# Masked self-attention over 16 batches on one core: the first batch's work placed by a plan written for it, and a new order at the end of the last batch

## The chip, the cores and the metric
The kernel runs on one core of a Trainium2 chip. The metric is the device time of one execution in microseconds (us), as a median of several runs. TensorE is called PE below, its weight loads PEld, VectorE DVE, ScalarE ACT, GpSimd POOL, and SyncE, which issues most of the transfers, SP.

## The reference
```python
xt = transpose(x, (0, 2, 1))              # x: 16 batches x 512 x 1024 tokens
qh = heads(xt @ Wq.T)                     # 8 heads of 64; queries, keys and values are all qh
scores = 0.125 * einsum('bhqd,bhkd->bhqk', qh, qh)
logits = (scores * cmask + (1 - cmask) * -1e30) * rmask      # one 0/1 mask, by column and by row
ctx = einsum('bhqk,bhkd->bhqd', softmax(logits), qh)
return x + transpose(ctx @ Wo.T, (0, 2, 1))
```
A token whose mask is 0 is no key for anybody. As a query its logits are all 0, so its context is the plain mean of all 1024 values, one row for the whole batch. The masks are drawn with about half the tokens active.

## The kernel before
**What is tiled.** The host hands in x also by token. On the core, the batches are ranked by their number of active tokens, and of each only the active tokens (up to 512, 528 or 544, padded) are gathered, 128 rows at a time, by an indirect transfer on POOL's queue (`rows`, L419). Batch 0 uses 512 columns, batches 1 to 4 use 544, later ones 528, the last two 512. The passive tokens need only the mean of x over all tokens. For it x is loaded once more by channel (`load_half`, `load_all`, L446 and L461) and summed along the tokens, for batches 0 and 1 in eight halves of 128 x 512, by ACT with an accumulator (`sum_half`, L456).

**Precision.** Matrices stand as a high and a low half-precision part, so that a product is three matmuls (high x high, low x high, high x low).

**The steps of a batch.** `xt` (L507) transposes gathered rows on PE; ACT writes the high part xh, DVE the low part xl. `query` (L536) makes a quarter e of q for half g of the tokens, 12 matmuls. ACT copies it out; DVE zeroes padding in place (L554), and `qsplit` (L562) makes the parts hl on DVE, from which four SP transfers build the operand xx (`spread`, L579). `value` (L600) transposes q to v; for batch 0 by PE transposes of q, later by matmuls on xx. The sums of squares of v give a bound on each head's scores: `peaks`, `top`, `bottom` (L656 to L697), with two small PE steps; the exponentials take the negative bound nm as their bias. `scores` (L741) does one pair of heads p for half the rows u, 8 matmuls (16 for a wider batch) into four PSUM banks, then four ACT exponentials that free these banks (L788). `attend` (L795) multiplies by v, 32 recorded matmuls; `recip_sums` and `recip_rows` (L839, L857) make reciprocals of the sums: a PE transpose, a DVE copy to rr (L867), a transfer to DRAM and two broadcasting transfers back into rb. `norm` (L890) multiplies by rb and splits into high and low on DVE. `product`, `project` (L923, L939) multiply by Wo, in units of three matmuls for each pair p, DVE adds x, and POOL scatters the rows to the output (`scatter_now`, L998).

**The order.** One stage of `run` (L1041) holds the scores of one batch, and between them the rest of the batch before and the preparation of the next. Its 18 steps S are the (p, i) of the batch with two empty ones; scores are issued for even i. Work is put between them by `fill` (L1270): from batch 1 on, by a table `plan` of steps; for batch 0, from a list m with costs, dealt out by shares (L1266 to L1281). From batch 1 on PE's order is exactly that of the code (`manual_schedule`, L1181); in batch 0 a scheduler orders PE. ACT and DVE are ordered by the scheduler throughout, and each engine does its instructions strictly in that order. `free` holds further calls by step: loads, sums, reciprocals, normalisations. Before batch 0's scores stands a setup (L1081 to L1153): masks are ranked, Wq and Wo are split (`split`, L183; the low part of Wo in `wide_rest`, L1131), the first rows are gathered, and the first quarters of q and v of batch 0 are made. PE runs dummy matmuls there (`warm`). `permute` (L215) orders the mask of batches 2 to 15 in one go, in batch 0.

**The end.** `last` (L1010) does what is left of the last batch: reciprocals and attention of its last pair 3, `norm_part` for that pair in two halves, and the projection of four chunks of 128 rows. The products of the pairs 0 to 2 are put ahead, as they do not need the last normalisation: 1 + 3 + 3 + 1 units for chunks 0 to 3 before it, then pair 3 of chunks 0 and 1, two units of chunk 3, and pair 3 of chunks 2 and 3. The normalisation of pair 2 is issued by `free` at the last step (L1309).

Of the kernel before, what the change touches and what calls it, by code (L numbers as in the profile page):

```python
# [47 lines left out]
class Fast:  # L48
# [166 lines left out]
    def permute(self, b0, b1):  # L215
# [3 lines left out]
        each = self.sb([P, n, TB, B], F16, "ch", 2)  # L219
# [226 lines left out]
    def load_half(self, b, k, after=None):  # L446

        c, h = k // 2, k % 2
        if k == 0:
            self.source(b)  # L450
        t = self.sb([P, T // 2], F32, *((("xm", 2), ("ub", 3), ("xi", 8), ("xi", 8))[k // 2 if b < 2 else 0]))
        src = self.x_nat[bass.ds(self.st[b]["row"], 1), c * P:(c + 1) * P, h * T // 2:(h + 1) * T // 2].rearrange("o p t -> (o p) t")
        self.once(self.nc.sync.dma_start(out=t, in_=src), after)
        self.st[b]["xm"].append(t)

    def sum_half(self, b, k):  # L456
        s = self.st[b]
        with self.behind(*self.exp):
            self.nc.scalar.activation(s["xm"][k], s["xm"][k], AF.Copy, accum_out=s["ms2"][:, k:k + 1])  # L459
# [397 lines left out]
    def recip_rows(self, b, p):  # L857
# [8 lines left out]
        with self.tc.high_priority(offset=HPO):  # L866
            self.spot_reads += [nc.vector.tensor_copy(rr, pt[:10]).ins] * spot  # L867
# [142 lines left out]
    def last(self, b):  # L1010
# [13 lines left out]
        self.recip_rows(b, 3)  # L1024
        self.attend(b, 3)
        self.attend_tail()
        self.product(s["ch"], s["cl"], chunk(0), pos[0], range(2, 3))
        for i in (1, 2):
            self.product(s["ch"], s["cl"], chunk(i), pos[i], range(3))
        self.product(s["ch"], s["cl"], chunk(3), pos[3], range(1))  # L1030
# [6 lines left out]
        self.product(s["ch"], s["cl"], chunk(3), pos[3], range(1, 3))  # L1037
        for i in (2, 3):
            self.project(b, i, pos[i], range(3, DC))

    def run(self, flag):  # L1041
# [71 lines left out]
        self.warm(13)  # L1113
        for k in range(3):
# [3 lines left out]
        for k in range(2 * DC):  # L1118
            self.load_half(0, k, self.pe)
# [7 lines left out]
        def half1(k):  # L1127
            with self.behind(*[self.last_xx] * (k > 2)):
                self.load_half(1, k, self.beat)

        def wide_rest():  # L1131
            with self.behind(self.last_hl):
                for f in wide:
                    f()
# [10 lines left out]
        first += [(0, index1)] + value(0, 0) + g1[:1] + query(0, 1, 1)[:1] + g1[1:2]  # L1145
        first += [(0, L(self.sum_half, 0, k)) for k in range(2 * DC)]
        first += value(0, 1) + query(0, 2, 0) + g1[2:3] + query(0, 2, 1)[:1] + g1[3:4]
        first += [(0, shift0), (0, wide_rest)]
        for _, f in first:
            f()  # L1150
        with self.behind(self.st[0]["top"]):
            for _, f in query(0, 1, 1)[1:] + query(0, 2, 1)[1:]:
                f()  # L1153
# [11 lines left out]
        def permute():  # L1165
            with self.behind(self.last_hl):
                self.permute(2, B)

        self.paced = True
        begin = g1[4:] + [(1.5, lambda: None)] + query(0, 3, 0) + value(0, 2) + query(0, 3, 1)  # L1170
        begin += xt(1)[:2] + value(0, 3)
        begin += [(0, apart(self.range_x, 0, c)) for c in range(DC)]
        groups = [(2, 4), (4, 8), (8, 11), (11, B - 2), (B - 2, B)]
        todo, carry = [], []
        if True:
            stack = ExitStack()
            for b in range(B + 1):
                o, n = b - 1, b + 1
                if b == 1:
# [21 lines left out]
                if n < B:  # L1201
                    q, x, v = (lambda e, g: query(n, e, g)), xt(n)[2 if b == 0 else 0:], (lambda e: [(0.25, L(self.value, n, e))])
# [7 lines left out]
                    if b:  # L1210
                        pre = [(0, L(self.active, *g)) for g in new[0]]
# [11 lines left out]
                    else:  # L1223
                        m = sums + x + pk(b, 1)
                        for g in new[0]:
                            m += [(0, permute), (0, L(self.active, *g))]
                        m += q(0, 0) + tp(b, 1) + bt(b, 1) + q(0, 1)
                        for g in new[0]:
                            m += [(0.3, L(self.slots, *g))]
                        m += hot + q(1, 0) + q(1, 1) + tc(0) + v(0) + index + take  # L1230
                        m += rng[:2] + tv(0) + rng[2:] + q(2, 0) + v(1)
                        m += q(2, 1) + pk(n, 0) + tp(n, 0) + q(3, 0) + bt(n, 0)
                        m += q(3, 1) + v(2) + tc(1) + [(0, L(self.means, n))]
# [13 lines left out]
                if b == 0:  # L1247
                    m = begin + m
# [12 lines left out]
                if b == 0:  # L1261
                    for k in range(2 * DC):
                        free.setdefault(k // 2, []).append(lambda k=k: half1(k))
                        free.setdefault(3 + k // 2, []).append(L(self.sum_half, 1, k))

                share = [(0, 0) if i is None else ((0, 0.3), (0.4, 0.4), (1.3, 1.3), (1.2, 1.2))[i] for _, i in S]  # L1266
                unit = sum(c for c, _ in m) / sum(map(sum, share)) if b == 0 else 0
                done, goal, pos = 0.0, 0.0, 0

                def fill(st, half):  # L1270
                    nonlocal done, goal, pos
                    if b:
                        for _, f in plan.get((st, half), []):
                            f()
                        return
                    part, end = share[st][half], st == N - 1 and half == 0
                    goal += part * unit
                    while pos < len(m) and (end or (part and done + m[pos][0] / 2 <= goal)):
                        m[pos][1]()
                        done += m[pos][0]  # L1280
                        pos += 1  # L1281

                for st, (p, i) in enumerate(S):
# [14 lines left out]
                    if b == 0 and p == 0 and i == 2 and self.wide[b] > 512:  # L1298
                        self.tail_scores(b, 0)

# [159 lines left out]
```

## Time and profile before
| | us |
|---|---|
| median of 3 runs (979.9, 980.95, 984.29) | 980.95 |
| the profiled execution | 984.38 |
| its span, first to last instruction | 982.7 |
| PE busy | 939.4 |
| DVE busy | 715.4 |
| ACT busy | 650.3 |
| POOL busy | 310.3 |

The busy times are those of the profiled execution. In a row of the timeline stand the start, the time of one or of several merged instructions, engine, line, operation and tiles, and in brackets how long the engine had been idle and what ended that. In a row of windows stand the stretch, its length, an engine's busy time with its number of instructions, the granted clock of PE (1.00 is full), the share of the transfer engines and the rate in GB/s.

### The profile page before, as it was taken

How to read it: one execution, taken by the hardware profiler on the slowest of the kernel's cores; microseconds unless marked ns; L12 is line 12 of the kernel's file. 1: busy time of each engine (PE TensorE's matmuls, PEld its weight loads, DVE VectorE, ACT ScalarE, POOL GpSimd, SP SyncE). 2: the span in 40 equal slices, each digit the busy share in tenths (PEclk: the TensorE clock that was granted, in tenths of full speed). 3: DMA queues.
4: the chain of work that ended last, by engine and by line, in shares of the span. 5: the costliest groups of instructions: out<-in, count | busy, mean ns of one | idle time of the engine just before them, and what ended most of it. 6: DMA issues, size and time to landing. Idle time of an engine off the chain costs nothing. (4 is left out here: it accounts for less than half of the span.)

```text
span 982.7 us, 22820 instructions
## 1 busy us (share of the span) xinstructions
PE 939.4 (96%) x8124; PEld 583.5 (59%) x8124; DVE 715.4 (73%) x2425; ACT 650.3 (66%) x1685; POOL 310.3 (32%) x309
## 2 busy tenths in 40 slices
PE   6787999999999999999999999999999999999997
PEld 4444656656666665666666666666666656565543
DVE  7687676777776786877688777777877678785663
ACT  4777666657766676776767678665767667565651
POOL 2201013124151342505234241432515135243452
PEclk9999999999999999999999999999999999999999
DMA  5747455567566577656657777654757747555552
GB/s 165 226 134 200 111 136 174 163 190 218 129 200 187 180 203 201 208 150 197 185 175 222 198 228 222 179 169 136 205 177 237 221 134 210 136 164 171 162 174 99
DMA packets 79145, 176.30 MB, mean 179 GB/s; under 512 B 14545, under 2 KB 22481, under 8 KB 79025
## 3 DMA queue, kind: packets, MB, share of 16 engines
q1 hardware_dynamic: 57968, 107.09, 38.9%
q0 software_dynamic: 21056, 67.68, 21.9%
q8 instruction: 66, 1.08, 0.5%
q14 instruction: 55, 0.44, 0.1%
HBM read 91.36 MB, written 33.91 MB: 127 GB/s over the span
## 5 line engine op out<-in xcount | busy, mean ns | idle before, releaser
L788 ACT ACTIVATE p<-pss,nm 128x528 f32<-128x528 f32 (+2 forms) x512 | 354.4, 703 | 101.1 <-PE pss L773 92.6
L808 PE MATMUL pss<-p,v 128*64 128x264 f32 (+2 forms) x2048 | 244.9, 392 | 0.0
L773 PE MATMUL pss<-xx 128*128 128x118 f16 (+17 forms) x1856 | 215.9, 290 | 7.8 <-ACT p L788 5.2
L1000 POOL DMA_INDIRECT y_out<-xa,idx x68 | 84.4, 1242 | 413.3 <-DVE nq L685 97.5
L808 PEld LDWEIGHTS pss<-p,v 128*64 128x64 f32 x2048 | 142.3, 138 | 88.6 <-issue 8.4
L773 PEld LDWEIGHTS <-xx 128*128 128x128 f16 (+1 forms) x1856 | 103.0, 97 | 91.3 <-issue 36.4
L547 PE MATMUL pm<-xh,wqh 128*128 128x264 f16 (+5 forms) x512 | 142.3, 278 | 2.7 <-DVE rr L867 0.8
L547 PE MATMUL pm<-xh,wql 128*128 128x264 f16 (+5 forms) x512 | 141.5, 276 | 0.0
L547 PE MATMUL pm<-xl,wqh 128*128 128x264 f16 (+5 forms) x512 | 141.5, 276 | 0.0
L422 POOL DMA_INDIRECT xa<-x_in,idx x68 | 75.7, 1113 | 125.9 <-DMA xx<-hl 47.0
L547 PEld LDWEIGHTS <-wqh 128*128 128x128 f16 x1024 | 97.1, 98 | 30.4 <-issue 11.4
L788 ACT ACTIVATION_READ_ACCUMULATOR p<-pss,nm 128x1 f32 x512 | 105.3, 206 | 0.0
L931 PE MATMUL pm<-woh,ch 128*128 128x512 f16 x240 | 91.1, 380 | 0.0
L931 PE MATMUL pm<-woh,cl 128*128 128x512 f16 x240 | 90.9, 379 | 0.0
L931 PE MATMUL pm<-wol,ch 128*128 128x512 f16 x240 | 90.9, 379 | 0.0
L551 ACT ACTIVATE q<-pm 128x264 f32<-128x264 f32 (+5 forms) x128 | 50.9, 398 | 46.9 <-PE pm L547 46.7
L937 DVE SCALAR_TENSOR_TENSOR xa<-pm,xa 128x512 f32<-128x512 f32 x61 | 41.6, 682 | 48.7 <-PE pm L931 48.1
L1000 POOL DMA_INDIRECT y_out<-xi,idx x60 | 64.6, 1077 | 35.7 <-PE pss L719 14.4
L614 ACT COPY v<-pm 128x512 f32<-128x512 f32 x64 | 37.5, 586 | 55.1 <-PE pm L610 54.3
L931 PEld LDWEIGHTS <-ch 128*128 128x128 f16 x480 | 44.9, 98 | 47.5 <-issue 4.1
L422 POOL DMA_INDIRECT xi<-x_in,idx x60 | 59.2, 986 | 22.5 <-issue 15.2
L459 ACT ACTIVATE xm<-xm 128x1024 f32<-128x1024 f32 (+1 forms) x60 | 62.3, 1041 | 3.6 <-DMA xm<-x_nat_in 3.6
(230 smaller groups left out, 1461.8 us busy)
## 6 DMA issues: line engine op xcount, KB each, us to landing
xm<-x_nat_in SPq DMA_DIRECT2D x56, 512.0 KB
xx<-hl SPq DMA_DIRECT2D x208, 136.0 KB
rb<-rd SPq DMA_DIRECT2D x72, 132.0 KB
xx<-hl SPq DMA_DIRECT2D x48, 128.0 KB
pt<-c SPq DMA_DIRECT2D x36, 132.0 KB
pt<-p SPq DMA_DIRECT2D x36, 132.0 KB
rb<-rd SPq DMA_DIRECT2D x32, 136.0 KB
ub<-ud SPq DMA_DIRECT2D x16, 256.0 KB
```

Of the source, the lines that this page charges most:

```text
L422: dma = self.nc.gpsimd.indirect_dma_start(out=tile[:n], out_offset=None, in_=self.x, in_offset=bass.IndirectOffsetOnAxis(ap=idx, axis=0))
L459: self.nc.scalar.activation(s["xm"][k], s["xm"][k], AF.Copy, accum_out=s["ms2"][:, k:k + 1])
L547: self.beat = nc.tensor.matmul(pq, lhsT=w[:, c, e * P:(e + 1) * P], rhs=xx[:, c, cols], start=(k == 0), stop=(k == 3 * DC - 1)).ins
L551: nc.scalar.activation(s["q"][:, e, cols], pq, AF.Copy, scale=1.0 / (SX * SW))
L614: nc.scalar.copy(v, pv)
L773: m = nc.tensor.matmul(flat[:, c0:c1], lhsT=w, rhs=x, start=banks[n] not in banks[:n], stop=banks[n] not in banks[n + 1:])
L788: e = nc.scalar.activation(t, flat[:, at:at + A], AF.Exp, bias=s["nm"][p // 2][:, p % 2 * 2 + k:p % 2 * 2 + k + 1], scale=SCALE, accum_out ...
L808: mm = nc.tensor.matmul(pav[k * DK:(k + 1) * DK, g], lhsT=s["v"][p][:, i, k * DK:(k + 1) * DK], rhs=ps[k, i][:, cols], start=(i == 3), sto ...
L931: mm = nc.tensor.matmul(po[:cols.stop - cols.start], lhsT=a[:, e, cols], rhs=w[:, e, :], start=(e == 0 and k == 0), stop=(e == DC - 1 and ...
L937: return self.nc.vector.scalar_tensor_tensor(x, po, 1.0 / (SX * SW), x, ALU.mult, ALU.add).ins
L1000: dma = self.nc.gpsimd.indirect_dma_start(out=self.out, out_offset=bass.IndirectOffsetOnAxis(ap=idx, axis=0), in_=x, in_offset=None)
```

## The change
- **Loads and sums of the first two batches.** The halves of x of batch 0 go to buffers of the tag `p` (exponentials). The first four loads of batch 0 wait for nothing on PE. The other four, and the first four of batch 1, are issued after the first transposes of batch 0 instead of after the third; the last four of batch 1 after the spread of batch 0's third quarter. Four of batch 0's sums are called ahead of its values, four after value 1. For batch 1 the sums of halves 4 to 7 are made by DVE (`tensor_reduce`) and not by ACT.
- **Batch 0's order.** It gets a table `plan` like the other batches, PE's order there is that of the code, and its small PE steps use the spare PSUM bank. Quarter 1 of q is split right after value 1.
- **Moved out of batch 0.** `wide_rest` goes to the first four steps of batch 1. `permute` runs for each group of batches at the place where their masks are needed (batches 0, 2, 6, 9 and 12), with its buffer under the tag `hl`.
- **The end.** The normalisation of pair 2 comes after the copy to rr of pair 3 (`self.recip`). Ahead of the last normalisation stand 1 + 3 + 1 units of chunks 0 to 2; after it chunk 2 and then chunk 3 are finished one by one.

```diff
-        each = self.sb([P, n, TB, B], F16, "ch", 2)
+        each = self.sb([P, n, TB, B], F16, "hl", 2)
...
+        t = self.sb([P, C], F32, "p", 12)[:, :T // 2] if b == 0 else \
+            self.sb([P, T // 2], F32, *((("xm", 2), ("ub", 3), ("xi", 8), ("xi", 8))[k // 2]))
...
+            if b == 1 and k > 3:
+                    self.nc.vector.tensor_reduce(s["ms2"][:, k:k + 1], s["xm"][k], AX.X, ALU.add)
+                return
...
+            self.recip = nc.vector.tensor_copy(rr, pt[:10]).ins
...
         self.recip_rows(b, 3)
+        with self.behind(self.recip):
+            self.norm(b, 2)
...
-        for i in (1, 2):
-            self.product(s["ch"], s["cl"], chunk(i), pos[i], range(3))
-        self.product(s["ch"], s["cl"], chunk(3), pos[3], range(1))
+        self.product(s["ch"], s["cl"], chunk(1), pos[1], range(3))
+        self.product(s["ch"], s["cl"], chunk(2), pos[2], range(1))
...
-        self.product(s["ch"], s["cl"], chunk(3), pos[3], range(1, 3))
-        for i in (2, 3):
-            self.project(b, i, pos[i], range(3, DC))
+        self.product(s["ch"], s["cl"], chunk(2), pos[2], range(1, 3))
+        self.project(b, 2, pos[2], range(3, DC))
+        self.product(s["ch"], s["cl"], chunk(3), pos[3], range(3))
+        self.project(b, 3, pos[3], range(3, DC))
...
+        for i in range(DC):
+            self.load_half(0, i)
         for k in range(3):
...
-        for k in range(2 * DC):
-            self.load_half(0, k, self.pe)
+            if k == 0:
+                for i in range(DC, 2 * DC):
+                    self.load_half(0, i, self.pe)
+                for i in range(DC):
+                    self.load_half(1, i, self.pe)
...
-        first += [(0, index1)] + value(0, 0) + g1[:1] + query(0, 1, 1)[:1] + g1[1:2]
-        first += [(0, L(self.sum_half, 0, k)) for k in range(2 * DC)]
-        first += value(0, 1) + query(0, 2, 0) + g1[2:3] + query(0, 2, 1)[:1] + g1[3:4]
-        first += [(0, shift0), (0, wide_rest)]
+        first += [(0, index1)] + sums0[:4] + value(0, 0) + g1[:1] + query(0, 1, 1)[:1] + g1[1:2]
+        first += value(0, 1) + split1 + sums0[4:] + query(0, 2, 0) + g1[2:3] + query(0, 2, 1)[:1] + g1[3:4]
+        first += [(0, shift0)]
...
-                if b == 1:
+                if b == 0:
                     self.spots = True
                     stack.enter_context(self.tc.manual_schedule(engines={mybir.EngineType.PE}))
...
-                        pre = [(0, L(self.active, *g)) for g in new[0]]
+                        pre = [(0, L(f, *g)) for g in new[0] for f in (self.permute, self.active)]
...
+                        plan = {(0, 0): g1[4:] + query(0, 3, 0) + value(0, 2) + rng0,
+                                (3, 0): query(0, 3, 1) + value(0, 3) + pk(b, 1) + x[:1],
+                                (5, 0): x[1:2], (5, 1): x[2:3],
+                                (7, 0): x[3:] + tp(b, 1) + q(0, 0) + bt(b, 1), (8, 1): pre,
+                                (9, 0): q(0, 1), (9, 1): q(1, 0) + post, (11, 0): hot,
+                                (12, 0): q(1, 1) + tc(0) + v(0) + rng[:2], (12, 1): index, (13, 0): take[:3],
+                                (14, 0): tv(0) + q(2, 0) + rng[2:], (14, 1): v(1) + q(2, 1) + pk(n, 0),
+                                (16, 0): q(3, 0) + tp(n, 0) + take[3:], (16, 1): q(3, 1),
+                                (17, 0): bt(n, 0) + v(2) + tc(1) + [(0, L(self.means, n))]}
...
-                            if p < 2 or b == B - 1:
+                            if p < 2:
```
In `plan`, q, x and v are the queries, transposes and values of batch 1, and the others those of batch 0.

62 lines of the change are left out of this document (19 added, 43 removed).

## The prediction
> **What bounds the kernel now.** I read the page first, then PE by stages, then the stage that stands out, then the waits and the timeline in it.
>
> ```profile
> span 982.7 us, 22820 instructions
> ```
> ```profile
> 31.60:105.00 73.40, 57.82 (x435) 0.91 0.60 163
> 105.00:930.00 825.00, 813.75 (x7238) 1.00 0.63 183
> ```
> From 105 to 930 us PE is idle for 11.3 of 825 us: there PE is the bound, and what PE gets done earlier by 105 should stay a gain to the end. From 31.6 (first scores of batch 0) to 105 (end of batch 0's last attention) 73.4 - 57.8 = 15.6 us are idle, and the clock is low. The same stretch by pieces:
>
> ```profile
> 45.40:48.40 3.00, 2.97 (x10) 0.50 0.75 226
> 58.80:62.10 3.30, 3.12 (x10) 0.50 0.57 149
> ...
> 92.90:95.80 2.90, 0.00 (x0) 1.00 0.72 182
> 95.80:102.90 7.10, 6.14 (x34) 0.54 0.36 83
> ```
> Three times PE ran at about half clock. That cost 2.97 x 0.5 + 3.12 x 0.5 + 6.14 x 0.46 = 5.9 us. With 15.6 idle, **21.5 us** is all that can be won there. Who caused the idle time:
>
> ```profile
> PE pss L773 <- ACT p L788: 5.0, 4, 3.1
> ...
> PE pm L670 <- DVE smcol L661: 2.2, 1, 2.2
> ```
> PE waits for exponentials to leave PSUM, for one spread, and for the bound before the first exponential. The chain of waits at the end holds only the last scatter, so the tail is taken from the timeline.
>
> **Part 1, the loads.** Before, SP held the first load until 20.36, behind PE's third transposes.
>
> ```profile
> 20.36 1.21 SPq L453 DMA_DIRECT2D xm<-x_nat_in  x2
> ```
> ```profile
> 16.14 0.60 ACT L477 ACTIVATE xh<-pss 128x512 f16<-128x512 f32 x1 [4.57 <-PE pss L519]
> ```
> In the changed build four loads wait only for their batch's number (about 7.5 us, an estimate), and ACT has four half sums in front of its first xh copy, which began at 16.14. Four loads issued by about 9.7 have 6.4 us to land and be summed. If they are late, all shifts 1:1; early they gain nothing by themselves, as PE's transposes wait for gathered rows. I take 0 (up to 5 lost, by the slowest load of the rows below).
>
> **Part 2, the bound.** The chain to the first exponential:
>
> ```profile
> 29.60 0.57 ACT L614 COPY v<-pm 128x512 f32<-128x512 f32 x1
> ...
> 33.67 0.62 ACT L593 ACTIVATE tmp<-v 128x512 f32<-128x512 f32 x1
> ...
> 37.07 0.69 ACT L788 ACTIVATE p<-pss,nm 128x512 f32<-128x512 f32 x1 [2.78 <-DVE nm L683]
> ```
> Value 1 was out of PSUM at 30.2, but ACT squared it only at 33.67, behind five half sums and two q copies; DVE's reduction, smcol and two PE steps follow. In the changed order the square stands right behind the copy. The copy itself comes 0.5 us earlier (no half sum ahead of q), so the square ends about 30.2, 4.1 us earlier. Then ACT still owes four sums (some 0.63 each, row 51.51 below) and two q copies, until 33.4. First exponential: 33.7, **3.3 us** earlier.
>
> **Part 3, batch 0's plan.** I walk PE through the eight score groups in the changed order, with these durations:
>
> ```profile
> 38.51 0.38 ACT L551 ACTIVATE q<-pm 128x256 f32<-128x256 f32 x1
> 38.77 0.59 ACT L614 COPY v<-pm 128x512 f32<-128x512 f32 x1
> 39.24 0.71 ACT L788 ACTIVATE p<-pss,nm 128x512 f32<-128x512 f32 x1
> ...
> 39.91 0.71 ACT L788 ACTIVATE p<-pss,nm 128x512 f32<-128x512 f32 x1
> ```
> ```profile
> 77.33 3.67 PE L808 MATMUL pss<-p,v 128*64 128x256 f32 x32
> ...
> 83.12 0.28 PE L547 MATMUL pm<-xh,wqh 128*128 128x272 f16 x1
> ...
> 84.40 0.28 PE L547 MATMUL pm<-xh,wql 128*128 128x272 f16 x1
> ```
> So, start to start on ACT, an exponential costs 0.67, a q copy 0.26, a v copy 0.47; on PE an attention 3.67, a query 84.40 - 83.12 + 0.11 = 1.4, and a score group some 1.6. A group may start only when the four exponentials of the one before are out. Idle PE that I find left:
> - Group 1 to 2: ACT needs 1.6 + 4 x 0.67 + 0.26 + 0.47 = 5.0 after the group's start and begins late (33.7); PE has 1.6 + 1.4 + 0.6 to do. Idle 1.5.
> - Group 2 to 3 has a **new wait**: DVE now does batch 1's half sums 4 to 7, and two of them stand ahead of the zeroing of q's last quarter, which value 3 needs; value 3 stands ahead of group 3 on PE. DVE is there at 39.5. Their loads go out behind the third spread, about 38.8 to 40.9. Rows for such a landing:
>
> ```profile
> 45.63 1.91 SPq L453 DMA_DIRECT2D xi<-x_nat_in  x4
> ```
> ```profile
> 51.51 0.63 ACT L459 ACTIVATE xi<-xi 128x512 f32<-128x512 f32 x1 [0.52 <-DMA xi<-x_nat_in]
> ```
> The second of these loads, issued about 46.4, had landed at 51.5: 5.1 us on busy queues. At 2.5 us the second lands at 42, at 5.1 at 44.5. Queued behind on DVE: this zeroing, the split of quarter 3, xl of batch 1. I take 42.4, DVE goes on at 43.0, idle 2.7 (bounds 0.3 and 5).
> - Group 4 to 5: `bottom` on PE now needs a maximum that stands behind two range reductions on DVE. Idle 1.2.
> - Group 6 to 7: fill of only 2.0 (a query, a value, the index) beside 3.5 us of ACT. Idle 1.5.
> - Before value 2 of batch 1, the spread:
>
> ```profile
> 87.12 1.71 PE L773 MATMUL pss<-xx 128*128 128x472 f16 x16
> ...
> 95.87 0.19 PE L610 MATMUL pm<-two,xx 128*128 128x64 f16 x1 [2.98 <-DMA xx<-hl]
> ```
> Before, its query ended where the row 87.12 begins, and the value came 8.8 us later. In the new order PE has 5.1 us of work there (a group, two queries, small steps), since batch 1's first scores moved behind it. At 8.2 us, idle 3.1.
> - Small ones: 0.5.
>
> Sum 10.5. The groups then start at about 31.9, 37.2, 44.2, 50.8, 56.8, 65.4, 70.5 and 79.5, value 2 at 87.4. The clock:
>
> ```profile
> 57.02 0.66 PE L519 MATMUL pm<-ident,xa 128*128 128x128 f32 x4 [1.23 <-DVE xl L478]
> 58.98 2.86 PE L773 MATMUL pss<-xx 128*128 128x512 f16 x8 [1.31 <-ACT p L788]
> ```
> The gaps of 3.1 (longest wait for L788) and 3.0 us (before 95.87), and these two of 1.2 and 1.3 with 0.7 of work between, were followed by half clock; the 2.2 for smcol was not. I count one half-clock spell, after the last gap, as costly as the one there before (2.8). So 13.3 of loss stays of 21.5: **8.2 us won** by 105, the 3.3 of part 2 within it. No row shows this order, so bounds: no spell and half of the gaps, 16; a spell of 2.8 after each of the five, 3 lost.
>
> The Trainium skill, page "TensorE: Matmul & The Clock Gate", section "What's actually happening", has the clock fall to half after one idle window of about 3.4 us. Here gaps of 2.98 and 3.08 us did it, so the trace is harsher. By the page none of the gaps left would do it; that is the first rival.
>
> **Part 4, what left batch 0.** The wide split (4 x 0.6 on DVE) comes back while DVE waits for value 2: 0. `permute`:
>
> ```profile
> 52.94 3.42 DVE L220 TENSOR_TENSOR ch<-c,given 128x1792 f16<-128x1792 f16 x1
> ...
> 60.74 2.00 DVE L223 TENSOR_REDUCE act<-ch 128x112 f16<-128x1792 f16 x1
> ```
> ```profile
> 167.14 0.29 DVE L478 SCALAR_TENSOR_TENSOR xl<-pm,xh 128x128 f16<-128x128 f32 x1 [0.16 <-ACT xh L477]
> ```
> ```profile
> 168.08 0.28 PE L547 MATMUL pm<-xh,wqh 128*128 128x274 f16 x1
> ```
> 3.42 + 2.00 for 1792 columns give 1.55 for 512 in batch 2, with the comparison 1.75; 1.3, 1.3 and 0.9 for the groups of batches 6, 9 and 12. In the build they stand ahead of the last xl (167.14, free at 167.4), which PE wants for the query from 168.2. 1.75 later is a wait of 0.95; with the same slack 0.5, 0.5 and 0.1 follow. DVE has idle time to catch up: I take **1.5 us lost** (0 to 5.2).
>
> **Part 5, the tail.**
>
> ```profile
> 962.73 0.33 PE L862 MATMUL pm<-ident,rcol 128*128 128x128 f32 x1 [0.23 <-DVE rcol L855]
> ```
> ```profile
> 963.05 0.69 DVE L913 TENSOR_TENSOR c<-c,rb 128x512 f32<-128x512 f32 x1 [0.38 <-DMA rb<-rd]
> 963.66 0.27 DVE L867 COPY rr<-pm 10x128 f32<-10x128 f32 x1
> ...
> 968.92 0.76 DVE L881 TENSOR_TENSOR c<-c,rb 128x256 f32<-128x256 f32 x2 [3.54 <-SPq L1430]
> ...
> 970.07 0.41 DVE L888 TENSOR_TENSOR xl<-c,xh 128x256 f16<-128x256 f32 x1
> ...
> 975.32 1.34 DVE L937 SCALAR_TENSOR_TENSOR xa<-pss,xa 128x512 f32<-128x512 f32 x2 [1.25 <-PE pss L931]
> ```
> ```profile
> 966.60 0.39 PE L931 MATMUL pm<-woh,xh 128*128 128x512 f16 x1
> ...
> 971.88 0.38 PE L931 MATMUL pm<-woh,xh 128*128 128x512 f16 x1
> ```
> ```profile
> 977.54 0.96 POOL L1000 DMA_INDIRECT y_out<-xa,idx  x1 [0.30 <-POOLq L1430]
> ```
> The copy to rr could start at 963.1, when the transpose ends, but stood behind the product L913: 0.55 earlier, and so are rb and 968.92. PE is full from 966.6 on, so this moves no end; it pays for the 3 units moved behind. Eight units took 971.88 - 966.60, 0.66 each; five last until 969.9, the third matmul wants the low half at 970.3, and that comes at 970.48 - 0.55. At the end chunks 2 and 3 were added one after the other (975.32, two in 1.34), and the last scatter began only when POOL was through with the one before (0.30 idle on its own queue). Now chunk 2 is added about 974 and its scatter gone; chunk 3's add still ends at 976.66, and its scatter begins 0.3 later, 976.96: 0.6 earlier, perhaps more as it has the transfers alone. **0.8 won** (0.3 to 1.1).
>
> **Sum.** -8.2 + 1.5 - 0.8 = -7.5 us. The profiled execution took 984.38 and would take 976.9; it lies 3.4 above the median of the runs, 980.95. I put the gain on the median: **973.5 us**.
>
> **Rivals.**
> - *The clock stays up* (chance 0.12). No spell of half clock: 2.8 more, 970.7; if the half sums also land before DVE asks, 2.4 more, 968.3. For it: the gaps are shorter than before. Against: three spells in this trace.
> - *New waits take the place* (0.18). The half sums land at 5 us (2.1 more), the following gap gets a half-clock spell (1.5), permute costs all of 5.2: 980.8. For it: the landing of 5.1 us. Against: twelve loads have gone by then, so the queues should hold less.
> - *Slower: PE's clock through batch 0* (0.14). Five gaps are left, and each may start a spell that costs 1.5 to 2.8. The sum is even when the spells cost 10.3, 20 us at half clock; all five at 2.8 give 984.7. For it: a pair of gaps of 1.2 and 1.3 sufficed before. Against: a gap of 2.2 did not.
> - *The change doesn't do what it says* (0.02): loads 0 to 3 land after 16 us and the sums in front of xh stop ACT; at 5 us late, 978.5.
>
> **How the numbers follow.** The forecast has 0.54, its own range 970.5 to 976.5. 966 to 982 takes in the rivals down to part of the third and leaves out some 0.1. A measurement of this kernel tells 0.5%, 4.9 us, from no change: below 976.05 lie most of the forecast and the first rival, 0.62; above 985.9 the worst of the third and what I have not thought of, 0.10; between, 0.28.
>
> **What would show it.** First exponential near 33.7 (part 2). A DVE wait for the loads L462 about 40 (new wait), a PE wait before group 3 released by DVE. Batch 0's last attention ending at about 96 to 97 instead of 104.8. A clock row of half rate only about 87 to 95. Waits of PE of up to 1 us for xl in batches 2, 6, 9 and 12. Last scatter 0.6 earlier against the PE end. Wrong if half sums or the clock hold PE more than 10 us in all, or if ACT sits before its first xh copy.

## The result, and the profile after

In the runs taken side by side the kernel before has a median of 982.39 us (10 runs), the changed one 976.21 us (10 runs): a ratio of 0.9938, 95% interval 0.9922 to 0.9955, or 6.1 us (4.4 to 7.7). The forecast was 973.5 us (966 to 982), 7.5 us less than before. A second set on the same level (the first run of the second group of experiments) gave 976.14 beside 981.27 us, a ratio of 0.9956 (0.9940 to 0.9972). A ratio here is not quite the quotient of the two medians beside it (0.9948 in this set).

The two profiled executions differ by 10 us, 984.38 to 974.4, more than the medians. Three rows of the profile before, on PE and ACT, say where most of the surplus comes from (columns: start, duration, engine and line, operation, in brackets the idle time ahead and what ended it):

```profile
786.39 1.06 ACT L459 ACTIVATE xm<-xm 128x1024 f32<-128x1024 f32 x1 [3.02 <-DMA xm<-x_nat_in]
...
787.45 0.68 ACT L724 ACTIVATE p<-pss,nm 128x528 f32<-128x528 f32 x1
```
```profile
788.28 2.12 PE L773 MATMUL pss<-xx 128*128 128x458 f16 x16 [2.42 <-ACT p L724]
```
A load of a later batch landed late, its sum held ACT for 3.02 us, the exponential behind it came late, and PE stood still for 2.42 us; 3.41 us at half clock followed (1.7 lost). That is 4.1 us which neither profile of the changed kernel has there; the change touches nothing at that place.

The changed kernel's span, and PE by stages, for the rows of before (columns: stretch, its length, PE busy with its number of instructions, granted clock, DMA share, GB/s):

```profile
span 972.7 us, 22828 instructions
```
```profile
31.60:95.00 63.40, 51.42 (x397) 0.95 0.58 158
95.00:920.00 825.00, 815.35 (x7265) 1.00 0.63 184
```
Idle from 31.6 to 95 are 12.0 us. The matmul right behind batch 0's last attention, first in the profile before and then in that of the changed kernel:

```profile
104.76 0.65 PE L719 MATMUL pss<-xx 128*32 128x272 f16 x16
```
```profile
98.15 0.65 PE L724 MATMUL pss<-xx 128*32 128x272 f16 x16
```
**6.6 us** are won by there. In the long middle PE is idle for 9.7 of 825 us; before, it was 11.3 with the 2.42 of the rows above. The waits of PE over 0.3 us between 31 and 105 us, in order of time, from its timeline:

```profile
33.56 1.13 PE L778 MATMUL pss<-xx 128*128 128x512 f16 x6 [1.30 <-DMA xx<-hl]
38.33 1.57 PE L778 MATMUL pss<-xx 128*128 128x512 f16 x8 [1.79 <-ACT p L793]
42.40 0.33 PE L612 MATMUL pm<-ident,q 128*128 128x128 f32 x1 [0.84 <-ACT q L556]
44.74 0.33 PE L612 MATMUL pm<-ident,q 128*128 128x128 f32 x1 [2.01 <-DVE q L559]
56.87 0.28 PE L552 MATMUL pm<-xh,wqh 128*128 128x272 f16 x1 [0.94 <-DVE xl L483]
...
73.11 0.34 PE L333 MATMUL pss<-oht,tmp 128*128 128x9 f16 x8 [1.50 <-DVE oht L279]
82.50 0.36 PE L615 MATMUL pm<-two,xx 128*128 128x64 f16 x7 [1.83 <-DMA xx<-hl]
90.90 0.38 PE L685 MATMUL pss<-ident,m 128*128 128x4 f32 x2 [0.49 <-DVE m L678]
91.69 0.36 PE L615 MATMUL pm<-two,xx 128*128 128x64 f16 x7 [0.36 <-DMA xx<-hl]
```
Against before, the long waits for exponentials (5.0 in all) are down to 1.79, and the wait for the bound (2.23 us before) is down to 0.34, at 30.95. New is the wait for q of value 3 (44.74) by way of DVE, as forecast, and at 82.50 one for a spread, at value 1 and not at value 2 as forecast. The wait at 33.56 is new too, and was not forecast. DVE's side of the first:

```profile
42.24 0.69 DVE L462 TENSOR_REDUCE ms<-xi 128x1 f32<-128x512 f32 x1 [3.20 <-DMA xi<-x_nat_in]
43.80 0.69 DVE L462 TENSOR_REDUCE ms<-xi 128x1 f32<-128x512 f32 x1 [0.87 <-DMA xi<-x_nat_in]
44.40 0.28 DVE L559 TENSOR_TENSOR q<-q,hr 128x128 f32<-128x128 f32 x1
```
Two half sums wait for their loads (3.20 and 0.87 us), and the zeroing of q stands behind them.

The tail: the transpose of the last reciprocals, and the last scatter.

```profile
953.33 0.33 PE L867 MATMUL pm<-ident,rcol 128*128 128x128 f32 x1 [0.23 <-DVE rcol L860]
```
```profile
967.53 0.96 POOL L1006 DMA_INDIRECT y_out<-xa,idx  x1 [1.63 <-DVE xa L943]
```
The scatter begins 14.20 us behind the transpose. Before it was 977.54 - 962.73 = 14.81.

### The profile page after: what moved, and what is told of

It reads as the page before. It is cut to its first block, busy times and chain, and to the rows that moved or that the text cites. A ratio compares the mean times of both kernels' runs of the same rounds, so it can differ in the third digit from the quotient of the medians.

```text
span 972.7 us, 22828 instructions
## 1 busy us (share of the span) xinstructions
PE 936.1 (96%) x8124; PEld 582.3 (60%) x8124; DVE 718.3 (74%) x2441; ACT 648.6 (67%) x1677; POOL 304.8 (31%) x309
## 4 chain that ended last, share of the span: by engine, by line
PE 82%; DVE 7%; DMA 4%; ACT 4%; issue 2%; SPq 1%; POOL 0%; POOLq 0%; DVEq 0%; ACTq 0%
PE pss L813 21%; PE pss L778 17%; PE pm L937 17%; PE pm L552 16%; ACT p L793 2%; PE pss L831 2%; DMA xx<-hl 2%; PE pm L524 2%; PE pss L724 1%; DMA xa<-x_in,idx 1%; PE pm L615 1%; DVE xl L483 1%; PE pss L937 1%; DVE xa L943 1%; PE pm L867 1%
## 5 line engine op out<-in xcount | busy, mean ns | idle before, releaser
L1006 POOL DMA_INDIRECT y_out<-xa,idx x68 | 81.9, 1205 | 409.0 <-DVE nq L690 84.8
L778 PEld LDWEIGHTS <-xx 128*128 128x128 f16 (+1 forms) x1856 | 103.4, 96 | 85.0 <-issue 35.1
L422 POOL DMA_INDIRECT xa<-x_in,idx x68 | 72.8, 1071 | 127.8 <-DMA y_out<-xa,idx 43.7
L943 DVE SCALAR_TENSOR_TENSOR xa<-pm,xa 128x512 f32<-128x512 f32 x61 | 41.6, 682 | 46.1 <-PE pm L937 45.6
L836 ACT COPY c<-pss 128x528 f32<-128x528 f32 (+2 forms) x64 | 38.3, 598 | 41.9 <-PE pss L831 26.4
```

Source lines behind the costliest of these rows:

```text
L422: dma = self.nc.gpsimd.indirect_dma_start(out=tile[:n], out_offset=None, in_=self.x, in_offset=bass.IndirectOffsetOnAxis(ap=idx, axis=0))
L778: m = nc.tensor.matmul(flat[:, c0:c1], lhsT=w, rhs=x, start=banks[n] not in banks[:n], stop=banks[n] not in banks[n + 1:])
L836: self.context_out = nc.scalar.copy(c[:, :A].rearrange("p (g c) -> p g c", g=2), pav).ins
L943: return self.nc.vector.scalar_tensor_tensor(x, po, 1.0 / (SX * SW), x, ALU.mult, ALU.add).ins
L1006: dma = self.nc.gpsimd.indirect_dma_start(out=self.out, out_offset=bass.IndirectOffsetOnAxis(ap=idx, axis=0), in_=x, in_offset=None)
```

## The experiments

Twelve runs, one of them of the changed kernel itself, each timed beside the kernel before on the same chip. The first four and the last four ran on chips where the kernel before takes 992 to 997 us, and PE's waits behind 105 us are longer for all of them, so a ratio is compared with others of its own group (the last run is a group by itself); up to 105 us the traces are compared directly. The changed kernel itself was timed in the second group alone. As a landmark serves the matmul right behind batch 0's last attention (98.15 in the first profile of the changed kernel).

**The tail alone.** The kernel before with these parts of the change and nothing else:

```
+            self.recip = nc.vector.tensor_copy(rr, pt[:10]).ins
...
+        with self.behind(self.recip):
+            self.norm(b, 2)
...
+        self.product(s["ch"], s["cl"], chunk(2), pos[2], range(1, 3))
+        self.project(b, 2, pos[2], range(3, DC))
+        self.product(s["ch"], s["cl"], chunk(3), pos[3], range(3))
+        self.project(b, 3, pos[3], range(3, DC))
...
-                            if p < 2 or b == B - 1:
+                            if p < 2:
```

> The kernel before with the change's last batch alone (copy of the reciprocals first, last two chunks one by one). Theory: from the last transpose of the reciprocals to the end of the span the profile of before has 982.7 - 962.73 = 19.97 us and the changed one 972.7 - 953.33 = 19.37, so this alone gives 0.6 us: a ratio of 0.9994, stretch near 19.4. Rival (the tail is held by PE, which is full there): 0.0, stretch near 20.0. Rival (the tail carries part of what the two profiles differ beyond batch 0): 2 us or more.

Ratio 0.9985 (0.9956 to 1.0013), which tells nothing at this size. The trace does:

```profile
977.78 0.33 PE L862 MATMUL pm<-ident,rcol 128*128 128x128 f32 x1 [0.23 <-DVE rcol L854]
```
```profile
991.98 0.96 POOL L1001 DMA_INDIRECT y_out<-xa,idx  x1 [1.63 <-DVE xa L938]
```
The scatter begins 14.20 us behind the transpose, the same as in the changed kernel: up to there the tail gives its 0.6 us, on its own. The span's end, however, comes 19.82 us behind the transpose, only 0.15 earlier than before, for from the scatter's start to the end it takes 5.62 us here (5.16 before, 4.65 to 5.31 in the other twelve profiles). How much of the 0.6 us reaches the end is not shown by this run.

**The bound late again.**

```
-        first += [(0, index1)] + sums0[:4] + value(0, 0) + ...
+        first += [(0, index1)] + value(0, 0) + ...
-        first += value(0, 1) + split1 + sums0[4:] + query(0, 2, 0) + ...
+        first += sums0 + value(0, 1) + query(0, 2, 0) + ...
-            for _, f in query(0, 2, 1)[1:]:
+            for _, f in split1 + query(0, 2, 1)[1:]:
```

> The changed kernel with batch 0's half sums all in front of value 1 again and the split of quarter 1 behind the bound, as before. Theory: the bound is what sets batch 0's start: first exponential back from 34.7 to about 37.0, all later groups with it, end of batch 0's last attention 98.2 + 2.3 = 100.5, time 2.3 us up (about 978.5). Rival: the spread of quarter 1 sets the start, and the loads and DVE set group 3, so that the 2.3 us are absorbed in waits that are there anyway: end of the attention below 99, time up by less than 0.7.

```profile
36.63 0.69 ACT L793 ACTIVATE p<-pss,nm 128x512 f32<-128x512 f32 x1 [3.02 <-DVE nm L688]
```
First exponential at 36.63 (34.1 to 35.5 in the changed kernel and the ten others that keep its start), held by the bound nm; landmark 103.05, ratio 0.9974 (0.9942 to 1.0006) beside 0.9937 and 0.9895 in the same group. The theory holds for the start: with the order of before, the bound sets it. The time does not show it, as the interval overlaps with that of the next run (0.9908 to 0.9966). The rival names the wrong spread: the first scores (`scores` takes xx of its own pair) read quarter 0 alone, and quarter 1's spread leaves SP only at 38.64 here. The landmark moved by 4.9 us against the first profile of the changed kernel and by 3.0 against the second (100.09, below), more than 2.3, as PE ran 10.2 us on end at half clock here (34.4 to 44.6). The wait on DVE before value 3 was absent, so a part was indeed absorbed, as the rival said, but not the whole.

**The half sums later on DVE.**

```
             if b == 1 and k > 3:
-                with self.nc.allow_low_precision(...):
+                with self.behind(self.last_hl), self.nc.allow_low_precision(...):
```

> The changed kernel with batch 1's half sums 4 to 7 on DVE behind the split of batch 0's quarter 3 instead of in front of its zeroing. Theory: the PE wait of 2.01 us before group 3 goes, and with it the half clock from 46.1 to 49.5 that follows it (1.7): 2.0 to 3.7 us won, about 973, group 3 starts near 43.3 instead of 45.3. Rival: DVE only passes the wait on: four sums of 0.69 now stand in front of xl of batch 1, PE waits for it at batch 1's first query (0.94 there now, up to 3.7 then), and the time stays within 0.7 us or rises.

The wait before group 3 is gone, and the first attention starts at 46.10 (48.40 in the changed kernel). The landmark is 98.48 all the same, and the ratio, 0.9937 (0.9908 to 0.9966), shows no clear gain. PE does not wait for xl more than in the changed kernel (0.93, there 0.94). Two waits for spreads are left:

```profile
79.47 0.36 PE L615 MATMUL pm<-two,xx 128*128 128x64 f16 x7 [1.65 <-DMA xx<-hl]
...
90.56 0.53 PE L615 MATMUL pm<-two,xx 128*128 128x64 f16 x7 [3.13 <-DMA xx<-hl]
```
The first, at value 1, was in the changed kernel too (1.83). New is the second: at 90.56, value 2 of batch 1, PE stands for 3.13 us for a spread (0.36 in the changed kernel), the wait that the forecast had there. So the rival had the right outcome and the wrong place, and a third theory was needed: **the end of batch 0 hangs on the chain from query 2 of batch 1 over DVE's split and the spread to value 2**, and what is won ahead of it is waited off there. What makes that spread slow comes out below, at the last two gathers.

**Query 2 ahead of value 1.**

```
-  (14, 0): tv(0) + q(2, 0) + rng[2:], (14, 1): v(1) + q(2, 1) + pk(n, 0),
+  (14, 0): tv(0) + q(2, 0) + rng[2:], (14, 1): q(2, 1) + v(1) + pk(n, 0),
```

> The changed kernel with query 2's second half in front of value 1 of batch 1. Theory: 1.4 us of PE work fill the wait of 1.83 us for the spread at 82.5, and without a long gap the half clock from 83.7 to 87.1 (1.7) does not come: about 3 us won, near 973, no clock row below 1 between 80 and 92. Rival: the wait only moves, since value 1, its square and batch 1's bound come later: PE waits for the bound (0.49 now) up to 2, and the time changes by less than 1 us. Second rival: the clock's spell has nothing to do with this gap and stays: 1.4 won at most.

```profile
79.37 0.36 PE L615 MATMUL pm<-two,xx 128*128 128x64 f16 x7 [0.27 <-DMA xx<-hl]
83.57 0.33 PE L675 MATMUL pss<-ident,smcol 128*128 128x128 f32 x1 [0.77 <-DVE smcol L669]
86.29 0.36 PE L615 MATMUL pm<-two,xx 128*128 128x64 f16 x7 [0.83 <-DMA xx<-hl]
92.75 0.65 PE L724 MATMUL pss<-xx 128*32 128x272 f16 x16
```
Waits of 0.27 and 0.83 us at the two values, no half clock from 28 to 110 us, landmark 92.75, ratio 0.9895 (0.9849 to 0.9942). From the first attention (45.98) to the landmark it takes 46.8 us, in the changed kernel 98.15 - 48.40 = 49.8: the 3 us expected; the other 2.4 us of the landmark were won ahead of the first attention, where the swap changes nothing. The swap fills one gap and also brings query 2's spread forward, which the third theory asks for: its first transfer leaves SP at 81.94, 1.62 us ahead of the last two gathers, and it is used 4.35 us later.

**The changed kernel again** (no edit).

> The changed kernel itself once more, as a base for the runs beside it. Theory: the gain is made in batch 0 and the tail, so it is the same number of us whatever the level of the chip: 6 us, ratio near 0.994, with the waits before group 3 and for the spread of value 1 of batch 1 there again, each 1 to 3 us, and half clock behind those that reach 1.8. Rival: the waits for transfers were chance in the one profile: neither of the two over 0.7.

Ratio 0.9956, as said above. The waits sit elsewhere than in the first profile: 0.60 on DVE at value 3, none at value 1, 3.08 at value 2:

```profile
44.40 0.33 PE L612 MATMUL pm<-ident,q 128*128 128x128 f32 x1 [0.60 <-DVE q L559]
...
88.15 0.19 PE L615 MATMUL pm<-two,xx 128*128 128x64 f16 x1 [0.73 <-DMA xx<-hl]
91.42 0.53 PE L615 MATMUL pm<-two,xx 128*128 128x64 f16 x7 [3.08 <-DMA xx<-hl]
96.49 3.67 PE L813 MATMUL pss<-p,v 128*64 128x256 f32 x32
100.09 0.65 PE L724 MATMUL pss<-xx 128*32 128x272 f16 x16
```
So two profiles of one kernel have the long wait at different places. Of the seven profiles of kernels that keep this order of values and queries and leave value 2 alone, six have the long wait at value 2 (2.8 to 3.3 us). PE was at half clock for four stretches of 3.41 us here, for two in the first profile, and the landmark is at 100.09. The expectation had waits of 1 to 3 us before group 3 and at value 1; neither reached 0.7, as its rival said.

**Useless matmuls in two gaps.** The values they write are overwritten by the transposes and matmuls behind them.

```
+                for _ in range(20 if k == 3 and e == 3 else 0):
+                    nc.tensor.matmul(pv[:, k, :], lhsT=self.on16, rhs=self.on16, start=True, stop=True)
...
+                for _ in range(20 if b == 1 and e == 1 and k == 0 else 0):
+                    nc.tensor.matmul(pv[:, k, :], lhsT=self.on16, rhs=self.on16, start=True, stop=True)
```

> The changed kernel with 20 small matmuls without use (128 columns each) put on PE into each of two gaps: in front of the last transpose of batch 0's value 3, and in front of value 1 of batch 1. They change no wait. Theory: the half clock comes from the idle stretch itself, so both spells (46.1 to 49.5 and 83.7 to 87.1 in the profile of the changed kernel, 1.7 us each) stay away: 1.7 to 3.4 won, clock 1.00 from 31 to 95. Rival (the clock falls by chance or by load, not by idle PE): the spells stay, time within 0.7 us or up by what the 40 matmuls cost (0.06 each, 2.4 at most).

Inconclusive: neither gap was long in this run, and half clock came at two other places (35.1, and 89.7 to 96.6 behind a wait of 2.98 at value 2). Landmark 100.44, ratio 0.9962 (0.9947 to 0.9976).

**The gathers later.**

```
-  (12, 1): index, (13, 0): take[:3],
+  (12, 1): index,
-  (14, 1): v(1) + q(2, 1) + pk(n, 0),
+  (14, 1): v(1) + q(2, 1) + pk(n, 0) + take[:3],
```

> The changed kernel with the first three gathers of batch 2 behind value 1 and query 2 of batch 1 instead of in front. Theory: the spread that value 1 waits for shares its queues with these gathers (issued 74.7, landed 82.4, gathers issued 75.3 to 78.7): alone it lands in some 4.5 us, the wait of 1.83 at value 1 goes and the half clock behind it (1.7); the gathers then meet the spread of value 2 instead, whose wait (0.36) grows to 1 to 3: in sum 0 to 3 won. Rival: the spread needs its 7.7 us alone as well: the wait at value 1 stays, 0 won.

The wait at value 1 is gone; value 2 waits 3.02, landmark 98.66, ratio 0.9954 (0.9935 to 0.9972). As expected, with nothing won in sum. That the repeat had no wait at value 1 either, with the gathers in their old place, is no objection: its value 1 came 7.3 us behind the first transfer of the spread (80.17 - 72.88). Here it came 5.7 us behind it (78.66 - 72.93) and found its data, while in the six profiles that do wait there, with the gathers at 0.6, 1.8 and 3.1 us behind that transfer, it took 7.3 to 7.8 us. So the spread is slower beside these gathers.

**The loads earlier.**

```
+        for k in range(DC, 2 * DC):
+            with self.behind(self.last_xx), self.tc.high_priority(offset=HPO):
+                self.load_half(1, k, self.beat)
         with self.behind(self.st[0]["top"]):
             for _, f in query(0, 2, 1)[1:]:
...
-                        if k >= DC:
-                            free.setdefault(0, []).append(lambda k=k: half1(k))
```

> The changed kernel with the loads of batch 1's half sums 4 to 7 issued in front of batch 0's third spread instead of behind it, at about 33 instead of 39.6. Theory: DVE's half sums find their data, the wait of 2.0 before group 3 goes and the half clock behind it (1.7): 2 to 3.7 won, group 3 starts near 43.3. Rival: the loads now share the queues with the third spread and the second, group 1 or value 2 of batch 0 waits for its spread instead: 0, or up to 2 lost.

DVE's wait shrinks to a PE wait of 0.63, the first attention starts at 45.85, the first group waits 1.49 for its spread (1.30 in the changed kernel), and yet: 1.62 at value 1, 3.25 at value 2, landmark 98.42, ratio 0.9949 (0.9933 to 0.9964). The first theory's local gain came, its sum did not: again waited off at value 2.

**Useless matmuls before value 2.**

```
+                for _ in range(40 if b == 1 and e == 2 and k == 0 else 0):
+                    nc.tensor.matmul(pv[:, k, :], lhsT=self.on16, rhs=self.on16, start=True, stop=True)
```

> The changed kernel with 40 small matmuls without use (128 columns, about 0.06 us each, 2.4 in all) on PE in front of value 2 of batch 1, where five of the six profiles of kernels in this order have a wait of 2.8 to 3.3 us for its spread and then 5 to 7 us at half clock. The wait itself cannot change. Theory (idle PE takes the clock down): no half clock from 87 to 98, 2.5 to 3.5 us won, near 973. Rival (the clock falls for another reason, as the load on the chip): half clock there all the same, time within 0.7 us of 976.

No half clock at all from 28 to 110, where the comparable runs had 3.4 to 6.8 us of it behind this wait; landmark 97.49 (100.09 in the repeat), the wait itself still there (2.4 us of matmuls, then 1.69 idle). So filling the idle time kept the clock up behind this wait; with the count in the last section this speaks for idle PE as what takes the clock down. Two things were chance here: the stretch around the wait held 1.72 us of work, an amount that was followed by half clock in other runs, and the half clock near 35 and 72 that the repeat had is absent, where nothing was filled. The ratio, 0.9976 (0.9949 to 1.0002), does not show the gain: on this chip the kernel is idle for 24 us between 105 and 875 in the profile of this run (the repeat above: 9), and the interval is 5 us wide.

**The last two gathers later.**

```
-  (16, 0): q(3, 0) + tp(n, 0) + take[3:], (16, 1): q(3, 1),
-  (17, 0): bt(n, 0) + v(2) + tc(1) + ...
+  (16, 0): q(3, 0) + tp(n, 0), (16, 1): q(3, 1),
+  (17, 0): bt(n, 0) + v(2) + take[3:] + tc(1) + ...
```

> The changed kernel with the last two gathers of batch 2 (issued at 85.8 and 87.1 in the repeat) behind value 2 of batch 1. Theory: they share the queues with the spread that value 2 waits for (issued from 85.1, landed 91.4, 6.3 us); alone it lands in 4.4 as in the first profile of the changed kernel (87.34 to 91.69, gathers only from 89.7): the wait of 3.1 becomes 1.2, and the half clock behind it goes with it or shrinks: 2 to 4 us won. Rival: what holds the spread is the broadcast of the reciprocals and the load of 512 KB behind it, which stay: 0.

In the repeat the last two gathers went out on POOL 0.7 us behind the first transfer of the spread that value 2 waits for, which left SP at 85.08; here they go out 2.3 us behind it (still ahead of value 2). The rows of the repeat, then those of this run:

```profile
85.08 0.47 SPq L586 DMA_DIRECT2D xx<-hl  x1
```
```profile
85.75 1.02 POOL L422 DMA_INDIRECT xa<-x_in,idx  x1 [7.41 <-ACT p L793]
87.07 0.88 POOL L422 DMA_INDIRECT xt<-x_in,idx  x1 [0.30 <-issue]
```
```profile
86.88 0.95 POOL L422 DMA_INDIRECT xa<-x_in,idx  x1 [0.70 <-ACT p L793]
88.13 0.88 POOL L422 DMA_INDIRECT xt<-x_in,idx  x1 [0.30 <-issue]
```
```profile
84.54 0.47 SPq L586 DMA_DIRECT2D xx<-hl  x1
...
86.34 0.59 SPq L589 DMA_DIRECT2D xx<-hl  x1
```
```profile
88.88 0.36 PE L615 MATMUL pm<-two,xx 128*128 128x64 f16 x7 [1.09 <-DMA xx<-hl]
```
First issue to use of the spread: 88.88 - 84.54 = 4.3 us instead of 91.42 - 85.08 = 6.3. The wait is 1.09, no half clock, landmark 95.34, ratio 0.9956 (0.9932 to 0.9979), in one group with the 0.9976 above. The theory holds: 1.7 us of distance from the gathers were worth 2 us of landing, and the broadcast and the load behind the spread, which stayed, were not what held it. The other traces bear it out: of the twelve profiles with a plan for batch 0, the seven in which the next gather goes out 0.7 or 0.8 us behind the spread's first transfer have its use 6.1 to 6.5 us behind that transfer, the five with 1.6 to 4.1 us have it 4.3 or 4.4 us behind. The first profile of the changed kernel (2.3 and 4.35) is one of the five, the repeat one of the seven: that is where their waits at value 2 differ.

**The swap with the early loads** (both diffs from above).

> The changed kernel with query 2's second half in front of value 1 of batch 1, and with the loads of batch 1's half sums 4 to 7 in front of the third spread. Theory: the end of batch 0's attention hangs on the chain query 2, split, spread, value 2 of batch 1; a gain ahead of it is lost in the wait for that spread unless this chain is earlier too. The swap starts it about 2 us earlier, so now the loads' gain is kept as well: attention of batch 0 ends near 92.5 (98.2 to 100.2 in the two profiles of the changed kernel), 5 to 7 us won, near 970. Rival (the low time of the swap alone was the noise of its chip): attention ends after 97, time within 1 us of 976.

Landmark 95.58, ratio 0.9907 (0.9879 to 0.9935), the best of its group. The wait at value 2 is 0.82. The 92.5 was missed, because two stretches of half clock (35.4 to 38.8, 72.9 to 76.3) came that the single swap did not have. By the landmark the rival is out. Against the changed kernel's ratios (0.9938 and 0.9956, from other chips) 3 to 5 us are won, not the 5 to 7 expected.

**All together**: the swap, the early loads, the last gathers late, and useless matmuls before batch 2's index and before value 2:

```
+        for _ in range(16 if b == 2 else 0):
+            self.spotted(nc.tensor.matmul(pi, lhsT=self.on16, rhs=self.on16[:, :NB], start=True, stop=True))
...
+                for _ in range(10 if b == 1 and e == 2 and k == 0 else 0):
+                    nc.tensor.matmul(pv[:, k, :], lhsT=self.on16, rhs=self.on16, start=True, stop=True)
```

> The changed kernel with query 2's second half in front of value 1 of batch 1, the four loads in front of the third spread, the last two gathers of batch 2 behind value 2, and small matmuls without use in two gaps (16 in front of batch 2's index, 10 in front of value 2). Theory: PE's clock is decided over fixed stretches of 3.41 us, where under about 1.6 us of PE work is followed by 3.41 us at half clock; no stretch from 45 to 105 falls under that now, and the chain to value 2 is early: attention of batch 0 ends at 91.5 to 93.5 (to 95.2 if the stretch around 31.5 to 35 falls under 1.6 us of work, which depends on where the stretches lie), 5 to 7 us less than the changed kernel, a ratio of 0.988 to 0.990. Rival: what batch 0 wins is waited off in batch 1 (gathers of batch 2 late, PE waits for them at 95 to 110): a ratio of 0.994 or more.

Ratio **0.9884** (0.9843 to 0.9925), landmark 93.57, one stretch of half clock up to there (34.2 to 37.6, the one left to chance). PE from 31.4 to 105 in this kernel:

```profile
31.40:105.00 73.60, 65.44 (x569) 0.98 0.60 164
```
and in the changed one:

```profile
31.40:105.00 73.60, 61.44 (x495) 0.95 0.57 155
```
PE is busy 4.0 us more in the same time (about 1 of it the useless matmuls), at a clock of 0.98 for 0.95. It beats the kernel before beyond the interval, and by its landmark the changed kernel, which was not timed beside it. The swap alone has a landmark of 92.75 and a ratio of 0.9895 (0.9849 to 0.9942), so nothing here shows that the other parts are needed beside it.

## Why the prediction was right, point by point

- *Part 1, loads: 0.* Right. ACT's four half sums ran from 12.15 to 15.1, and the first xh copy waited for PE, not for them:

```profile
16.34 0.60 ACT L482 ACTIVATE xh<-pss 128x512 f16<-128x512 f32 x1 [1.12 <-PE pss L524]
```
- *Part 2, the first exponential at 33.7.* It came at 34.73, 1.0 late. The bound was ready in time (nm from 32.06); but the first scores' spread, that of quarter 0, was there only at 33.56 (row above, 1.30 idle). Its first transfer left SP at 27.17, so it took 6.4 us; before, the first scores began 4.05 us behind it (31.64 - 27.59). When the bound was taken off the path, this spread was next in line, and the forecast had put no price on it. Why it took longer is open: a gather goes out 0.8 us behind it in both kernels.
- *Part 3, 8.2 won by the end of batch 0's attention.* 6.6 in the profile, 4.7 in the repeat: the right mechanism, and its size too high. Idle time was forecast as 10.5 us and came as 12.0 and 12.3: about right in sum, in part by luck, as misses of either sign offset each other. By place: 1.30 before the first scores, not forecast, 2.85 before group 3 (0.84 + 2.01; 2.7 forecast), 1.79 before group 2 (1.5), 1.50 at the index, by DVE and not by ACT (1.5), 0.94 for xl of batch 1, not forecast, 0.23 for the bound before group 5 (1.2). The spread before value 2 was 3.08 in the repeat (3.1 forecast); in the first profile it was 0.36, with 1.83 for another spread at value 1, which the forecast did not have. The groups started at 31.4, 38.3, 45.3, 53.2, 58.9, 68.3, 73.6 and 84.7; in the repeat, with group 3 less late, 57.0 and 66.4 stand against the forecast's 56.8 and 65.4.
- *The terms that were mis-sized are the idle time and the clock*: the idle time by 1.5 and 1.8; for the clock one spell, 2.8, was forecast, and there were two stretches in the first profile (3.4 us lost) and four in the repeat (5.7). The rule behind it, a gap of some 3 us or a pair of 1.2 and 1.3, was wrong; the last section has one that fits. "Half clock only about 87 to 95" was right in the repeat but for two stretches more, and wrong in the first profile (46.1 and 83.7).
- *Part 4, permute: 1.5 lost.* Smaller. In the middle PE waits for xl before a query in batches 2 and 6, for 0.44 and 0.25 us (0.43 and 0.70 in the repeat), and not in 9 and 12; a third wait of 0.17 stands before as well, where there was another of 0.18. So it cost 0.5 to 1.0. The sums of the middle, before and after:

```profile
PE pm L547 <- DVE xl L478: 0.3, 2, 0.2
```
```profile
PE pm L552 <- DVE xl L483: 0.9, 3, 0.4
```
  From landmark to the last transpose the changed kernel takes 855.2 (854.7 in the repeat), the one before 858.0, less the 4.1 of its stall 853.9: 0.8 to 1.3 longer, of the same size as the xl waits; the rest was not traced.
- *Part 5, the tail: 0.8 won.* 0.6 up to the start of the scatter, as forecast, and nothing on top; from there to the end takes 4.65 to 5.62 us from run to run.
- *Sum.* -6.6 + 1.3 - 0.6 = -5.9 in the first profile and -4.7 + 0.8 - 0.6 = -4.5 in the repeat; measured -6.1 and -4.3. That it agrees to 0.2 is in part luck: both sums lean on one profile of before, and the tail-alone run, whose batch 0 is that of before, has its landmark at 106.75, 2.0 later. The forecast's -7.5 had 1.6 to 3.5 too much from batch 0, in the first profile more from idle time than from the clock, in the repeat more from the clock, and gave some back by too dear a permute. Of the parts of the change, the tail and the order around the bound had runs of their own; what the plan of batch 0, the loads and permute did is read from the traces alone.
- *Rivals.* New waits did take a place of the old, at value 2, but that one was in the forecast. The slower rival's mechanism, clock spells, worked at half its price. The first rival, a clock that stays up, did not come in either profile; the rule behind it is taken up in the last section.

## What to carry to other kernels

A gain ahead of a transfer that PE must wait for in any case is waited off there: find the last such transfer in the stage (here the spread of query 2) and start its chain earlier, before the gaps ahead of it are closed. Three edits that each removed a wait gave nothing clear; moving one query ahead of one value brought the landmark from 98 to 100 down to 92.75. In time it is 0.9895 beside 0.9937 of the old order in one group, with intervals that overlap; with the early loads it is 0.9907 (0.9879 to 0.9935) beside 0.9976 (0.9949 to 1.0002), which do not. Look also at what goes out beside such a transfer: gathers 0.7 or 0.8 us behind its first part made it some 2 us longer. And a landing time read from one profile is one draw: two traces of the same kernel had their long wait in different places.

## What the runs showed of the hardware

PE's half clock came in pieces of 3.41 us or a whole multiple in every trace, but for the piece at the very end, and within a trace the pieces start at whole multiples of 3.41 us from each other (46.14 and 83.69 here: 11 x 3.41). Cut along these boundaries, PE's work in the changed kernel reads:

```profile
35.90:39.31 3.41, 1.62 (x12) 1.00 0.65 164
39.31:42.73 3.42, 2.58 (x20) 1.00 0.87 235
42.73:46.14 3.41, 1.40 (x9) 1.00 0.95 310
46.14:49.55 3.41, 3.41 (x16) 0.50 0.63 202
...
70.03:73.45 3.42, 1.92 (x28) 1.00 0.28 92
...
80.27:83.69 3.42, 1.59 (x21) 1.00 0.72 241
83.69:87.10 3.41, 3.41 (x14) 0.50 0.01 2
```
1.40 and 1.59 us of work in a stretch were followed by half clock in the next; 1.62 and 1.92 were not. Over all fourteen profiles cut in this way from 25 to 105 us, all 19 stretches with 1.59 us or less were followed by half clock; of the 20 from 1.62 to 1.81 eight were; from 1.88 on none was, but for three (2.0 to 2.5) that ran at half clock themselves. So a gap of 1.5 to 2 us can cost 1.7 us more when it falls into one stretch, and costs nothing more when a boundary cuts it: of the eleven profiles with 1.50 us idle at the index, three had half clock behind it. That a rerun moves the boundaries, and with them a few us, fits with the two profiles of the changed kernel; the run times were not split by it. The Trainium skill, page "TensorE: Matmul & The Clock Gate", section "What's actually happening", says that the window of about 3.4 us runs free of the kernel; the traces agree (pieces of 3.41 us, and boundaries of the first profile and the repeat, 46.14 and 72.32, that are 7.7 stretches apart). It calls the window before half clock idle, and the forecast had read this as a gap as long as the window; here a window less than about half busy sufficed.
